# Separate views of a table in DRAM for the rows of the last three blocks, and another rhythm for the block tails at the layer seams

## The chip, the cores and the metric

One core of a Trainium2 chip runs the kernel. Its engines work side by side, each through its own list of instructions in order: PE (TensorE, matrix products), DVE (VectorE), ACT (ScalarE), POOL (GpSimd, which here mainly issues indirect DMAs) and SP (SyncE, which issues plain DMAs). Engines wait for each other, and for DMAs, by semaphores. The metric is the device time of one execution in microseconds; a kernel is given by the median of several runs.

## The reference

A graph network of four layers over 8 batches of 2048 nodes with 128 features, and one adjacency matrix, in which an entry is set with probability 0.0078, so a node has some 16 neighbours. Layers 0 and 1 are attention with 8 heads, masked by the adjacency, with a feed-forward part and two layer norms; layers 2 and 3 are graph attention (GAT):

```python
# layers 0 and 1
Q, K, V = h @ Wq, h @ Wk, h @ Wv               # 8 heads of 16
scores = einsum('bnhd,bmhd->bhnm', Q, K) / sqrt(16)
scores = where(adj == 0, -inf, scores)
attn_out = einsum('bhnm,bmhd->bnhd', softmax(scores), V)
x = layer_norm(h + (attn_out @ Wo + bo))
x = layer_norm(x + relu(x @ W1 + b1) @ W2 + b2)
# layers 2 and 3
h = x @ W
e = leaky_relu((h @ a_src)[:, :, None] + (h @ a_dst)[:, None, :], 0.2)
att = nan_to_num(softmax(where(adj == 0, -inf, e)))
x = layer_norm(einsum('bij,bjd->bid', att, h) + x)
```

## The kernel before

**Sparse work in blocks.** The kernel first turns the adjacency into lists of neighbours. Nodes are sorted by their number of neighbours into 16 blocks of 128 (`perm` holds the order), so that a block needs as many neighbour slots as its largest node has; `CAPS` gives the slots of each block, falling from 29 to 10. For every layer there is a table in DRAM, `tables[l]`, with one row for each node: its keys and values (2048 floats) for layers 0 and 1, its projected features and score terms (1040 floats) for layers 2 and 3. The slots of a block are worked through in chunks of a few slots. `gather` (L288) fetches, for one slot, one table row for each of the 128 nodes, by an indirect DMA that POOL issues: 1 MB in layers 0 and 1, 0.53 MB in layers 2 and 3. The rows land in one of 7 buffers called `kv`.

**A chunk.** `attention_chunk` (L605): the DVE multiplies keys with queries (L613) and halves the product (L619), PE adds up (L296, tile `pair`), ACT takes exponentials (L635), PE turns them (L639), ACT copies them into `weights` (L643), the DVE multiplies values with weights (L651), PE accumulates in `acc` (L296). `gat_chunk` (L764) does the like: scores on the DVE (L781), ACT scaling (L798), DVE products and sums (L793, L804), PE accumulation.

**A block's tail.** When the last chunk of a block is accumulated, `outputs` (L674) scales it on the DVE and the tail finishes the layer for the block. `attention_tail` (L699, in two halves of four batches) and `gat_tail` (L811) go back and forth between PE, for the products and layer norms (L705 to L748, L827, L303), and ACT (L462, L469, L473, L732, L835). `project` (L492) multiplies the new state with the next layer's weights (L499), and ACT copies the result to the tile `rows` (L509, and L520 to L522 for the score terms of a GAT layer, the last of them to `own`). `state_done` (L524) then keeps the state by a plain DMA of SP and calls `put_rows` (L485): an indirect DMA of POOL that scatters the 128 rows of the block into `tables[l + 1]`. These are the puts.

**The seams between layers.** A chunk of the next layer may need rows of any block. To start before all 16 blocks are put, the first two blocks of layers 1 to 3 have lists of their own, `sorted_lists`, in which neighbours that lie in early blocks come first. `EARLY` (L47) says how many of the first slots can be gathered when all but the last 3, 2 or 1 blocks are put; `fetch` (L1108) computes from it `need`, the number of puts that a chunk's gathers must follow, and issues its gathers when `put[l]` has reached that. What remains of the lists is gathered with `need` 16; among this is the chunk called folded, whose slots follow through the plain `lists`, and which is the first of the new layer that needs the put of block 15. `ORDER` (L48) is the order of these early chunks.

**Dependencies.** The program is traced in order, and a tracker puts in the waits from what each instruction reads and writes. It sees a table as one thing. So a gather waits for every put issued before it, and a put waits for every gather of this table issued before it to have landed, though it writes other rows than these read. `clear_late` (L475) has written zeros into the rows of the last three blocks at the start, so gathers never read undefined memory.

**Order of the work.** `layers` (L1188) steps through the chunks in a fixed pipeline. At several points of a step it calls `slot` (L1133): this advances each running thread by one stage (they are generators), then each running tail by one stage, then calls `fetch`; on every third call the tails get a second stage if `hurry` (L1128) says so, which is in layers 2 and 3 before all 16 puts of the layer are issued, and at one block of layer 2. The place at which a stage is traced is its place in the order of every engine that it uses.

```python
    def hurry():
        c = every[min(now[0], len(every) - 1)]
        return c["l"] == 2 and c["t"] == NT - 1 or c["l"] > 1 and put[c["l"]] < NT
```

Of the kernel before, what the change touches and what calls it, by code (L numbers as in the profile page):

```python
# [7 lines left out]

# [11 lines left out]
NT = N // P  # L20
# [24 lines left out]


EARLY = (((8, 3), (12, 2), (16, 1)), ((8, 3), (12, 1)))  # L47
ORDER = {2: ((0, 0, 12), (1, 0, 8), (0, 12, 16), (1, 8, 12)),  # L48
         4: ((0, 0, 8), (1, 0, 8), (0, 8, 16), (1, 8, 12))}
SEG = 128  # L50
# [12 lines left out]
def cut(k, end, n):  # L63

    res = []
    for m in split(end - k, n):
        res.append((k, m, False))
        k += m
    return res


def pieces(l, n):

    done, res = [0] * NT, []
    if l > 0:
        for t, k, end in ORDER[n]:
            res += [(t, *c) for c in cut(k, end, n)]
# [10 lines left out]
def sparse_path(ctx: ExitStack, tc: tile.TileContext, ins: dict, out: bass.AP, flag: bass.AP):  # L88
# [10 lines left out]
    nc = tc.nc  # L99
# [50 lines left out]
    def buffer():  # L150
        turn[0] += 1
        return bufs[turn[0] % KVB]
# [118 lines left out]
    def width(l):  # L271
        return NB * (2 * D if l < 2 else D + 2)


    tables = [dram.tile([N + (l > 1), width(l)], F32, name=f"table{l}") for l in range(4)]

    x_rows = ins["x_nodes"]


# [5 lines left out]
        nc.sync.dma_start(xT.rearrange("p b n -> p (b n)"), kept[t])  # L285
        return xT

    def gather(l, index, dst):  # L288
        nc.gpsimd.indirect_dma_start(  # L289
            out=dst, out_offset=None, in_=tables[l][:, :],  # L290
            in_offset=bass.IndirectOffsetOnAxis(ap=index, axis=0),
            bounds_check=N - (l < 2), oob_is_err=False,
        )

    def turn_into(dst, src, start):
        nc.tensor.matmul(  # L296
            dst, src, ident, start=start, stop=True, is_transpose=True, skip_group_check=True
        )
# [83 lines left out]
    def order_lists(t):  # L382
# [27 lines left out]
        yield  # L410
        for i, b in EARLY[t]:
            late = small.tile([P, 1], F32, tag="late", name="late", bufs=1)
# [62 lines left out]
    def clear_late():  # L475

        rows = rows_of(blocks[0][0])
        nc.vector.memset(rows, 0.0)
        for l in (1, 2, 3):
            for t in range(NT - 3, NT):  # L480
                for _ in range(3):
                    yield
                put_rows(l, t, rows)

    def put_rows(l, t, rows):  # L485
        nc.gpsimd.indirect_dma_start(  # L486
            out=tables[l][:, :],
            out_offset=bass.IndirectOffsetOnAxis(ap=perm[:, t : t + 1], axis=0),
            in_=rows[:, : width(l)], in_offset=None,
        )  # L490
# [33 lines left out]
    def state_done(l, t, box):  # L524


        box["halves"] = box.get("halves", 0) + 1
        if box["halves"] == 2:
            if l < 3:
                nc.sync.dma_start(kept[t], box["x"].rearrange("p b n -> p (b n)"))  # L530
                put_rows(l + 1, t, box["rows"])
                put[l + 1] += 1
            box["done"] = True
            state(l, t + STATES)
# [164 lines left out]
    def attention_tail(l, t, box, i):  # L699
# [58 lines left out]
        yield from project(l + 1, i, xT, rows_of(box), t)  # L758
        yield
        state_done(l, t, box)  # L760


# [48 lines left out]
    def gat_tail(l, t, box):  # L811
# [33 lines left out]
        def half_rows(h):  # L845
            scaled(h)
            yield
            pt = transpose4(ns[h])
            yield
            affine(xT[:, 4 * h : 4 * h + 4, :], pt, wt["col"][:, 0:2])  # L850
            yield
            yield from project(3, 4 * h, xT, rows_of(box), t)
            yield
            state_done(l, t, box)
# [15 lines left out]
        if l == 3:  # L870
            for _ in range(3):
                yield
            nc.vector.tensor_mul(n, n, last_g[:, None, :].to_broadcast([P, B, D]))
            yield
            nc.vector.tensor_add(n, n, last_b[:, None, :].to_broadcast([P, B, D]))
            yield
            nc.gpsimd.indirect_dma_start(
                out=out, out_offset=bass.IndirectOffsetOnAxis(ap=perm[:, t : t + 1], axis=0),
                in_=n.rearrange("p b d -> p (b d)"), in_offset=None,
            )  # L880
            state_done(l, t, box)
            state_done(l, t, box)
# [207 lines left out]
    put = [NT, 0, 0, 0]  # L1090
    every = []
    blocks = [[{} for _ in range(NT)] for _ in range(4)]
    for l in range(4):
        per = 2 if l < 2 else 4
        for t, k, ns, folded in pieces(l, per):
            c = dict(l=l, t=t, k=k, ns=ns, folded=folded, box=blocks[l][t])
# [3 lines left out]
    now = [0, 0]  # L1100
    beat = [0]

    def advance(group):
        for g in list(group):
            if next(g, 0) == 0:
                group.remove(g)

    def fetch():  # L1108

        while now[1] < len(every):  # L1110
            c = every[now[1]]
            l, t, k, ns = c["l"], c["t"], c["k"], c["ns"]

            if now[1] - now[0] > (5 if now[1] >= KVB and every[now[1] - KVB]["l"] > 1 else 4):
                return
            resorted = l > 0 and t < 2 and not c["folded"]
            need = NT - max([b for end, b in EARLY[t] if k + ns <= end] + [0] if resorted else [0])
            if put[l] < need:
                return
            c["buf"] = buffer()[:, : ns * width(l)].rearrange("p (s c) -> p s c", s=ns)  # L1120
            c["turn"] = turn[0]
            for i in range(ns):
                at = t * BASE if resorted else first[t]
                index = (sorted_lists if resorted else lists)[:, at + k + i : at + k + i + 1]
                gather(l, index, c["buf"][:, i])
            now[1] += 1

    def hurry():  # L1128

        c = every[min(now[0], len(every) - 1)]  # L1130
        return c["l"] == 2 and c["t"] == NT - 1 or c["l"] > 1 and put[c["l"]] < NT

    def slot():  # L1133
        advance(threads)
        advance(tails)
        fetch()
        beat[0] += 1
        if beat[0] % 3 == 0 and hurry():
            advance(tails)

    def drain():
# [20 lines left out]
    def state(l, t):  # L1162
        if t >= NT:
            l, t = l + 1, t - NT
        if 0 < l < 4:
            blocks[l][t].update(x=load_state(t), ready=True)
# [21 lines left out]
    def layers():  # L1188
        threads.append(first_states((0,)))
        drain()  # L1190
        fetch()
        begin(every[0])
        for _ in weights:
# [4 lines left out]
        for i in range(len(every) + 2):  # L1198
# [3 lines left out]
            while added:  # L1202
                c2 = added.pop(0)
                go(c2)
                if c2["last"]:
                    threads.append(tail(c2["l"], c2["t"], c2["box"]))
            now[0] = i
            fetch()
            if c["k"] == 0:
                l, t = c["l"], c["t"]  # L1210
                if l == 0:
                    if t + 2 < NT:
                        threads.append(find_lists(t + 2))
                    if t == 0:
                        threads.append(first_states(range(1, NT)))
                        threads.append(later(12, clear_late))
                    if t in (2, 6):
                        threads.append(order_lists(t // 4))
                while l < 2 and "asked" not in c["box"]:
                    slot()  # L1220
            while i < len(every) and now[1] <= i:
                slot()
# [10 lines left out]
            if c1["l"] in (2, 3) and c1["last"]:  # L1233
                sums(c1["l"], c1["t"], c1["box"])
                threads.append(scales(c1["l"], c1["box"]))
            go(c)
            slot()
            go(c)
            slot()
# [541 lines left out]
```

## Time and profile before

| | |
|---|---|
| median of 3 runs | 2844.97 us (2840.76 to 2846.59) |
| the profiled execution | 2843.96 us |
| its span in the profile | 2842.2 us |
| granted clock of TensorE, mean | 0.934 |
| busy: DVE, PE, POOL, ACT | 2520.0, 2388.3, 1753.6, 1375.9 us |
| HBM traffic over the span | 356 GB/s |
| seam from layer 0 to 1 | about 1050 to 1150 us |
| seam from layer 1 to 2 | about 1915 to 1995 us |
| seam from layer 2 to 3 | about 2385 to 2455 us |
| puts (L486) | 57, of which 48 carry rows of layers 0 to 2 and 9 are the zeros of `clear_late` |

Times are microseconds from the start of the span. In a view of groups of instructions each line names the source line, the engine, the operation, the tiles written and read, the count, the busy time and the idle time of the engine just before, with what ended it. In a view in time order each line has the start, the duration, the engine and line, and in brackets the idle time before it and what ended that, its releaser. A DMA shows twice: as the instruction of the engine that issues it, and as the wait of those who need what it moves. A releaser is the semaphore event that came last by the profile; where the engine named had long been done, another of the things waited for was the true one.

### The profile page before, as it was taken

The numbers are of one execution on the slowest core, as the hardware profiler recorded it, in microseconds if no ns is written. First come the engines' busy times: TensorE is split into PE (matmuls) and PEld (weight loads), VectorE is DVE, ScalarE is ACT, GpSimd is POOL, SyncE is SP. The second block draws the span as 40 slices with busy tenths as digits, with TensorE's granted clock in tenths as the row PEclk, the third lists the DMA queues.
The fourth block names the chain that finished last, engine by engine and source line by source line (L and its number), as shares of the span: only waits on it lengthen the run. The fifth ranks groups of instructions, "written<-read, shape, count | busy, mean of one in ns | idle before, by whom it ended". The sixth has DMA issues, their size and how long they took to land.

```text
span 2842.2 us, 49663 instructions
## 1 busy us (share of the span) xinstructions
PE 2388.3 (84%) x18176; PEld 2180.7 (77%) x18176; DVE 2520.0 (89%) x2496; ACT 1375.9 (48%) x5021; POOL 1753.6 (62%) x1276
## 2 busy tenths in 40 slices
PE   5857898899899998699989999997667887788885
PEld 3656888788788887588878888886667787777885
DVE  8888999999899897899999999985889997699995
ACT  3511444454455554154445555565345565354554
POOL 1266688678656544646565665572776775677772
PEclk9987999999999999999999999999889888999998
DMA  9698889999989878789999999984999998899994
GB/s 364 243 376 334 350 330 342 383 331 348 377 324 375 309 303 336 301 307 372 351 379 353 351 377 346 350 306 171 374 411 385 408 408 316 319 411 413 407 413 171
DMA packets 197766, 982.15 MB, mean 346 GB/s; under 512 B 30284, under 2 KB 32076, under 8 KB 125520
## 3 DMA queue, kind: packets, MB, share of 16 engines
q0 software_dynamic: 172112, 885.12, 80.7%
q1 hardware_dynamic: 20502, 75.52, 6.8%
q10 hardware_dynamic: 4900, 18.24, 1.7%
q8 instruction: 147, 2.41, 0.3%
q14 instruction: 105, 0.86, 0.1%
HBM read 921.35 MB, written 91.55 MB: 356 GB/s over the span
## 4 chain that ended last, share of the span: by engine, by line
PE 43%; DVE 22%; DMA 15%; issue 8%; ACT 6%; POOL 1%; POOLq 0%; DVEq 0%; ACTq 0%
PE acc L296 15%; DMA kv<-table,lists 10%; DVE kv L613 7%; DVE kv L651 7%; PE pair L296 4%; PE m L748 4%; PE m L727 4%; DMA kv<-table,sorted_lists 3%; PE m L303 2%; PE m L499 2%; DVE kv L793 2%; PE m L591 2%; PE m L743 2%; DVE kv L619 2%; PE m L550 2%
## 5 line engine op out<-in xcount | busy, mean ns | idle before, releaser
L289 POOL DMA_INDIRECT kv<-table,lists x938 | 1301.2, 1387 | 672.4 <-PE acc L296 327.7
L296 PE MATMUL acc<-ident,kv 128*128 128x128 f32 x8048 | 1060.5, 286 | 171.6 <-DVE kv L651 87.8
L296 PEld LDWEIGHTS acc<-ident,kv 128*128 128x128 f32 x8048 | 964.4, 149 | 241.6 <-DVE kv L651 111.8
L651 DVE TENSOR_TENSOR kv<-kv,weights 128x2048 f32<-128x2048 f32 (+1 forms) x282 | 626.1, 2220 | 61.1 <-ACT weights L643 61.0
L613 DVE TENSOR_TENSOR kv<-kv,q 128x2048 f32<-128x2048 f32 (+1 forms) x280 | 618.0, 2207 | 55.2 <-DMA kv<-table,lists 35.9
L793 DVE TENSOR_TENSOR kv<-kv,pair 128x3584 f32<-128x3584 f32 (+1 forms) x150 | 530.7, 3538 | 0.9
L296 PE MATMUL pair<-ident,kv 128*128 128x128 f32 (+1 forms) x2256 | 302.9, 279 | 89.9 <-issue 67.2
L619 DVE TENSOR_TENSOR kv<-kv 128x1024 f32<-128x1024 f32 (+1 forms) x282 | 334.7, 1187 | 9.1
L296 PEld LDWEIGHTS pair<-ident,kv 128*128 128x128 f32 (+1 forms) x2256 | 259.0, 141 | 108.4 <-issue 80.8
L643 ACT COPY weights<-pair 128x128 f32<-128x128 f32 (+1 forms) x282 | 73.2, 260 | 385.0 <-PE pair L639 378.6
L289 POOL DMA_INDIRECT kv<-table,sorted_lists x150 | 192.9, 1286 | 104.6 <-PE acc L296 36.2
L798 ACT ACTIVATE kv<-kv,ws 128x128 f32<-128x128 f32 x544 | 174.7, 397 | 170.0 <-DVE ws L787 164.8
L462 ACT ACTIVATE n<-m,eps 128x128 f32<-128x128 f32 x512 | 181.1, 371 | 149.1 <-PE m L748 145.9
L635 ACT ACTIVATE ring<-pair 128x128 f32<-128x128 f32 (+1 forms) x282 | 77.8, 276 | 319.7 <-PE pair L296 244.9
L835 ACT ACTIVATE n<-m,eps 128x128 f32<-128x128 f32 x256 | 90.6, 373 | 177.6 <-PE m L827 175.5
L486 POOL DMA_INDIRECT table<-rows,perm x57 | 90.9, 1595 | 125.7 <-ACT own L522 35.3
L748 PE MATMUL m<-w_L_w,hT 128*128 128x128 f32 x1024 | 156.4, 275 | 0.0
L469 ACT ACTIVATE n<-m,rs 128x128 f32<-128x128 f32 x512 | 145.8, 374 | 0.1
L748 PEld LDWEIGHTS m<-w_L_w,hT 128*128 128x128 f32 x1024 | 135.2, 192 | 0.0
L727 PE MATMUL m<-n1T,w_L_gnn_W 128*128 128x512 f32 x256 | 132.0, 599 | 1.5 <-ACT hT L732 1.4
L303 PE MATMUL m<-ident,n 128*128 128x128 f32 x640 | 112.2, 291 | 12.5 <-ACT n L469 6.4
L499 PE MATMUL m<-w_L_h,xT 128*128 128x130 f32 x512 | 83.3, 294 | 40.0 <-ACT xT L473 25.8
(220 smaller groups left out, 3685.1 us busy)
## 6 DMA issues: line engine op xcount, KB each, us to landing
kept<-xT SPq DMA_DIRECT2D x48, 512.0 KB, 6.7
xT<-kept SPq DMA_DIRECT2D x48, 512.0 KB, 7.0
kv<-in_adj_dram SPq DMA_DIRECT2D x16, 1024.0 KB, 9.4
table<-kv ACTq DMA_DIRECT2D x16, 1024.0 KB, 5.2
kv<-table,lists POOLq DMA_INDIRECT x938, 8.6
kv<-in_x_nodes_dram SPq DMA_DIRECT2D x16, 512.0 KB, 6.6
kv<-table,sorted_lists POOLq DMA_INDIRECT x150, 7.1
found<-cand POOLq DMA_DIRECT2D x16, 64.0 KB, 6.1
```

Source lines behind the costliest of these rows:

```text
L289: nc.gpsimd.indirect_dma_start(out=dst, out_offset=None, in_=tables[l][:, :], in_offset=bass.IndirectOffsetOnAxis(ap=index, axis=0), bound ...
L296: nc.tensor.matmul(dst, src, ident, start=start, stop=True, is_transpose=True, skip_group_check=True)
L303: nc.tensor.transpose(pt[:, j * P : (j + 1) * P], src[:, j, :], ident)
L462: nc.scalar.activation(dst[:, i, :], z[:, i, :], AF.Square, bias=eps, scale=D**-0.5, accum_out=ss[:, i : i + 1],)
L469: nc.scalar.mul(dst[:, i, :], z[:, i, :], rs[:, i : i + 1])
L613: nc.vector.tensor_mul(kk, kk, q[:, None].to_broadcast([P, ns, NB, D]))
L619: nc.vector.tensor_add(hk.rearrange("p j (c h) -> p c j h", h=NH), kj[:, :, :NH, :], kj[:, :, NH:, :])
L651: nc.vector.tensor_mul(vv, vv, w.rearrange("p (s b h) -> p (s b) h", b=NB, h=NH)[:, :, None, :] .to_broadcast([P, ns * NB, HD, NH]),)
L727: nc.tensor.matmul(ph, wt["1"][:, f * P : (f + 1) * P], n1T.rearrange("p b c -> p (b c)"), start=True, stop=True,)
L748: nc.tensor.matmul(y[:, j, :], hT[:, f, j, :], wt["2"][:, f, :], start=False, stop=f == 1, skip_group_check=True,)
L793: nc.vector.tensor_mul(hv[:, :, :nv, :], hv[:, :, :nv, :], wc[:, :, :nv, None].to_broadcast([P, ns, nv, D]))
L798: nc.scalar.mul(hv[:, i, b, :], hv[:, i, b, :], ws[:, i, b - nv : b - nv + 1])
```

## The change

Two things are changed.

First, the tables of layers 1 to 3 get views which the tracker holds to be disjoint from each other, while the table itself still overlaps them all: view 0 for the rows of blocks 0 to 12, and one for each of the blocks 13, 14 and 15 (`LATE = 3`). Each view is the whole table as far as addresses go. `put_rows` writes through the view of its block. A gather with `need` under 16 reads through view 0, and is given by hand a dependency on the puts of those blocks from 13 on that it does need; a gather with `need` 16 reads through the table. With this, the puts of blocks 13 to 15 no longer wait for early gathers, and early gathers don't wait for puts that they don't need.

Second, `slot` advances the tails a second time on every call, not every third, while the layer of the current chunk is at least 1 and not all 16 puts of its table are issued. This holds at all three seams; `hurry` had held for layers 2 and 3.

```diff
@@ -3,6 +3,7 @@
 import concourse.bass as bass
 import concourse.tile as tile
 from concourse import mybir
+from concourse.ap import dram_disjoint_views
 from concourse.masks import make_identity
 from concourse._compat import with_exitstack
 
@@ -45,6 +46,7 @@
 
 
 EARLY = (((8, 3), (12, 2), (16, 1)), ((8, 3), (12, 1)))
+LATE = 3
 ORDER = {2: ((0, 0, 12), (1, 0, 8), (0, 12, 16), (1, 8, 12)),
          4: ((0, 0, 8), (1, 0, 8), (0, 8, 16), (1, 8, 12))}
 SEG = 128
@@ -274,6 +276,9 @@
 
     tables = [dram.tile([N + (l > 1), width(l)], F32, name=f"table{l}") for l in range(4)]
 
+    views = {l: dram_disjoint_views(tables[l][:, :], 1 + LATE) for l in (1, 2, 3)}
+    puts = {l: [] for l in (1, 2, 3)}
+
     x_rows = ins["x_nodes"]
 
 
@@ -285,12 +290,19 @@
         nc.sync.dma_start(xT.rearrange("p b n -> p (b n)"), kept[t])
         return xT
 
-    def gather(l, index, dst):
-        nc.gpsimd.indirect_dma_start(
-            out=dst, out_offset=None, in_=tables[l][:, :],
+    def gather(l, index, dst, need):
+        this = nc.gpsimd.indirect_dma_start(
+            out=dst, out_offset=None, in_=tables[l][:, :] if need == NT else views[l][0],
             in_offset=bass.IndirectOffsetOnAxis(ap=index, axis=0),
             bounds_check=N - (l < 2), oob_is_err=False,
         )
+        if need < NT:
+            for other in puts[l][NT - LATE : need]:
+                tc.add_manual_dep(
+                    this.ins, other.name,
+                    mybir.DependencyInfo(mybir.DependencyClass.Sync, mybir.DependencyReason.DATA),
+                    reason="rows of a block before",
+                )
 
     def turn_into(dst, src, start):
         nc.tensor.matmul(
@@ -482,9 +494,9 @@
                     yield
                 put_rows(l, t, rows)
 
-    def put_rows(l, t, rows):
-        nc.gpsimd.indirect_dma_start(
-            out=tables[l][:, :],
+    def put_rows(l, t, rows, dst=None):
+        return nc.gpsimd.indirect_dma_start(
+            out=tables[l][:, :] if dst is None else dst,
             out_offset=bass.IndirectOffsetOnAxis(ap=perm[:, t : t + 1], axis=0),
             in_=rows[:, : width(l)], in_offset=None,
         )
@@ -528,7 +540,9 @@
         if box["halves"] == 2:
             if l < 3:
                 nc.sync.dma_start(kept[t], box["x"].rearrange("p b n -> p (b n)"))
-                put_rows(l + 1, t, box["rows"])
+                dst = views[l + 1][max(0, t - (NT - LATE) + 1)]
+                assert len(puts[l + 1]) == t
+                puts[l + 1].append(put_rows(l + 1, t, box["rows"], dst).ins)
                 put[l + 1] += 1
             box["done"] = True
             state(l, t + STATES)
@@ -1122,7 +1136,7 @@
             for i in range(ns):
                 at = t * BASE if resorted else first[t]
                 index = (sorted_lists if resorted else lists)[:, at + k + i : at + k + i + 1]
-                gather(l, index, c["buf"][:, i])
+                gather(l, index, c["buf"][:, i], need)
             now[1] += 1
 
     def hurry():
@@ -1135,7 +1149,8 @@
         advance(tails)
         fetch()
         beat[0] += 1
-        if beat[0] % 3 == 0 and hurry():
+        c = every[min(now[0], len(every) - 1)]
+        if c["l"] > 0 and put[c["l"]] < NT or beat[0] % 3 == 0 and hurry():
             advance(tails)
 
     def drain():
```

## The prediction

> **What bounds the kernel.** I read the page first: which engine is busy, and where the traffic sinks.
>
> ```profile
> PE 2388.3 (84%) x18176; PEld 2180.7 (77%) x18176; DVE 2520.0 (89%) x2496; ACT 1375.9 (48%) x5021; POOL 1753.6 (62%) x1276
> ...
> GB/s 364 243 376 334 350 330 342 383 331 348 377 324 375 309 303 336 301 307 372 351 379 353 351 377 346 350 306 171 374 411 385 408 408 316 319 411 413 407 413 171
> ...
> L486 POOL DMA_INDIRECT table<-rows,perm x57 | 90.9, 1595 | 125.7 <-ACT own L522 35.3
> ```
>
> The DVE is the busiest engine at 89%, but the bandwidth row has a hole: 171 in its 28th slice, which is 1918 to 1990 us, where layer 1 ends and layer 2 begins. The last line is the puts (L486), the scatters of a finished block's rows into the next layer's table: 57 of them, with POOL idle 125.7 us before them. A put is cheap to issue, so what it waits for is the question. Next, busy time by stretch (PE, PEld, DVE, ACT, POOL, then clock, DMA share and GB/s):
>
> ```profile
> 1150.00:1250.00 100.00, 78.91 (x608) 70.12 (x609) 95.46 (x57) 31.58 (x114) 56.90 (x34) 0.94 0.85 312
> ...
> 1985.00:2350.00 365.00, 276.64 (x2010) 260.98 (x2011) 338.19 (x398) 190.72 (x758) 277.93 (x250) 0.85 1.00 394
> 2350.00:2445.00 95.00, 72.58 (x546) 68.20 (x545) 63.27 (x70) 51.14 (x205) 43.31 (x41) 0.86 0.76 283
> 2445.00:2790.00 345.00, 280.11 (x2322) 271.82 (x2321) 310.15 (x373) 162.65 (x632) 260.31 (x255) 0.94 1.02 408
> ```
>
> In layers 2 and 3 the gather stream is the limit (DMA share 1.00 and 1.02, 394 and 408 GB/s). At the seam from layer 2 to layer 3 the share drops to 0.76. At the start of layer 1 the DVE is the limit (95.46 of 100 us). Past each seam some resource is saturated, so what a seam gains or loses is passed on whole; what it gains is when the next layer's stream can start. Then POOL in time order at the seam from layer 2 to 3 (start, duration, line, idle before and its end):
>
> ```profile
> 2390.35 0.99 POOL L289 DMA_INDIRECT kv<-table,sorted_lists  x1 [0.30 <-issue]
> 2399.57 1.02 POOL L486 DMA_INDIRECT table<-rows,perm  x1 [8.22 <-DMA kv<-table,sorted_lists]
> 2403.74 1.01 POOL L289 DMA_INDIRECT kv<-table,sorted_lists  x1 [3.16 <-DMA table<-rows,perm]
> ...
> 2416.21 1.02 POOL L486 DMA_INDIRECT table<-rows,perm  x1 [7.57 <-ACT kv L798]
> 2420.38 1.01 POOL L289 DMA_INDIRECT kv<-table,sorted_lists  x1 [3.15 <-DMA table<-rows,perm]
> ...
> 2439.35 1.02 POOL L486 DMA_INDIRECT table<-rows,perm  x1 [8.90 <-DMA kv<-table,sorted_lists]
> 2443.49 1.01 POOL L289 DMA_INDIRECT kv<-table,lists  x1 [3.12 <-DMA table<-rows,perm]
> ```
>
> Puts of blocks 13, 14 and 15. Each sits until the early gathers in front of it have landed (8.22, 7.57, 8.90 us), then goes out into an empty queue, and the next gather waits for it to land (3.16, 3.15, 3.12). The releaser of the second is named ACT, but that had long been done; the gathers were outstanding. The rows themselves were ready sooner: the last ACT write (L522) ends at 2383.8, 2409.5 and 2427.3. The other two seams:
>
> ```profile
> 1136.66 2.53 POOL L486 DMA_INDIRECT table<-rows,perm  x1 [16.33 <-DMA kv<-table,sorted_lists]
> ...
> 1949.78 1.02 POOL L486 DMA_INDIRECT table<-rows,perm  x1 [15.96 <-ACT own L522]
> ...
> 1980.45 1.02 POOL L486 DMA_INDIRECT table<-rows,perm  x1 [16.44 <-ACT own L522]
> ```
>
> The first is block 15 from layer 0 to 1: it waits 16.33 us for gathers, with its rows ready at 1118.4. The next two, blocks 14 and 15 from layer 1 to 2, wait for something else: ACT's own last copy, ended 1949.6 and 1980.2. So at this seam it is the block's tail that is late. What the DVE loses behind them, again by its timeline:
>
> ```profile
> 1117.18 2.29 DVE L613 TENSOR_TENSOR kv<-kv,q 128x2048 f32<-128x2048 f32 x1 [4.18 <-DMA kv<-table,sorted_lists]
> ...
> 1149.54 2.29 DVE L613 TENSOR_TENSOR kv<-kv,qf 128x2048 f32<-128x2048 f32 x1 [7.79 <-DMA kv<-table,lists]
> ...
> 1992.75 0.17 DVE L781 TENSOR_TENSOR kv<-kv,mine 128x16 f32<-128x16 f32 x1 [17.18 <-DMA kv<-table,lists]
> ...
> 2450.92 0.17 DVE L781 TENSOR_TENSOR kv<-kv,mine 128x16 f32<-128x16 f32 x1 [8.08 <-DMA kv<-table,lists]
> ```
>
> and the puts' own view, what POOL waited for, who waited for the put, and its time to landing:
>
> ```profile
>   ACT own L522: 35.3, 3
>   DMA kv<-table,sorted_lists: 33.5, 3
> ...
>   ACT rows L509: 19.3, 3
> ...
> DMA to landing us min/median/max: 3.4/8.5/12.0
> ```
>
> A put alone lands 3.4 us after issue; those sent into a filled queue take 8.5 at the median, 12.0 at most.
>
> **The change, part by part.** Nothing is added on any engine: matmuls, DVE, ACT, POOL and SP instructions are as many as before, and DVE's and SP's order is the same. POOL's order differs at one seam only, layer 0 to 1: puts 14 and 15 each go ahead of 6 gathers. What changes besides is which waits the last three puts carry (before all eight gather lanes and ACT; after one lane and ACT) and the order of ACT and PE at the three seams.
>
> *Seam 2 to 3, the views.* Put 13 no longer waits 8.22 us and goes at 2391.65, right behind the gather of 2390.35 (1.30 us pace). But that gather's packets still stand in the same queue, and the put of before started only when they had landed, at 2399.5. In a filled stream a further 0.53 MB costs 1.3 us (411 GB/s), against 3.46 us for a put sent alone (2399.57 to 2403.03). So it lands at about 2401.0, 2.0 us sooner, not 8.2. ACT's L509 copy, held 7.88 us for this put until 2403.05, moves with it, so do the gathers of 2403.74 and rows 14. Put 14 gains the same on top (3.46 against 1.4), put 15 again: 2.0, 4.0, 6.0 us. The fold chunk of the DVE comes at 2444.9 instead of 2450.92. Bounds: nothing, if the queue keeps the fixed part anyway; 8.22 + 7.57 + 8.90 = 24.7 us, if puts pass the gathers in flight. I take 6.0: the 8.5 us median landing in filled queues is near the first case, far from the second.
>
> In the Trainium skill, "DMA: Bandwidth & Descriptors", section "Queues, rings and completion order", each DMA engine takes the descriptors of a ring in order. This speaks against the change: an early issue buys no place ahead of the gathers. By it the seam gives these 6.0 us; without it 24.7. The 8.5 us median agrees.
>
> *Seam 1 to 2, tails at two stages a beat.* Views give nothing here, since puts 14 and 15 wait for ACT's rows. PE was full from 1919 to 1972 and mixes the tails with the chunks' accumulations; in the new order 48 accumulating matmuls that stood ahead of block 15's last projection (L499) come behind it (24 for block 14). Twelve of them took 1.47 us at 1914.79, so 48 x 0.122 = 5.9 us. The put goes at 1974.5 and the stream starts 5.9 us sooner. The displaced matmuls run in PE's hole of 17 us while the DVE waits (17.18 us before 1992.75); were that hole gone, they would cost their 5.9. Bounds: 0, if the tail is a ping-pong of PE and ACT in which the matmuls only filled gaps; 17.18 is all that there is to lose. I take 5.9, as PE shows no gaps there.
>
> *Seam 0 to 1, both.* Here the stage behind is the DVE's. After 1098 the DVE waits 17.0 us in all: 2.17 + 1.19 for weights, 4.18 for gathers, 1.38 + 0.28, and 7.79 for the fold chunk behind put 15. Put 15 could go at about 1117 instead of 1136.66, so the data waits can go. Against it, the doubled tail pushes chunk work back on PE: 48 accumulations and 27 pair matmuls pass behind the tail, and the chunks' softmax sums (L639) come up to 12.7 us later in the middle of the seam (PE's order summed at 0.599 us for wide, 0.22 for narrow and 0.11 for accumulating matmuls), back to 0 at the end of it. PE is full from 1045 to 1119.7, so this is real delay, and weights (ACT) and DVE queue behind it. Laying DVE's unchanged order (5.69 us a chunk) against that, the fold chunk comes at 1147.8 instead of 1149.54: 1.7 us gained of 17.0. Bounds: 17.0 gained, if PE's lateness hides; 12.7 lost, if the waits stay. I take 1.7, the hand-laid order.
>
> Sum: 6.0 + 5.9 + 1.7 = 13.6 us. The profiled execution took 2843.96 (span 2842.2 and 1.8 around it) and comes to 2830.4; it lies 1.0 below the median of the runs, 2844.97, so I predict **2831**.
>
> **Rivals.**
> *A, the views bring nothing, the tails do.* A put's packets go out behind the gathers, and its fixed time still follows the last of them: seam 2 to 3 gives 0, seam 0 to 1 gives 0, only the 5.9 remain: 2839. For it: no row shows the fixed 3.4 us of a lone landing overlapped. Against: the three puts at seam 2 to 3 go out after the queue has run empty, and that at least ends.
> *B, puts overtake the gathers.* Seam 2 to 3 then gives the whole 24.7, with 5.9 and 1.7 that is 32.3: 2813. For it: the 8.5 us median may come from puts behind the 1 MB gathers of layers 0 and 1, and no row of before shows a put behind early gathers of 0.53 MB. Against: the same packets share one queue, and 12.0 us is the worst.
> *C, starved chunks: slower.* The tails' second stage comes before the chunks' matmuls, so weights come late and, as PE's accumulations are what POOL mostly waits on for free kv buffers (300 waits of L289, 363.9 us in the list of waits), the gathers too. Seam 0 to 1 then loses 12.7 with its waits still paid, seam 1 to 2 gives back its 5.9, and seam 2 to 3 keeps 6.0 less the 32 accumulations that go behind block 15's tail there (3.9): 12.7 - 2.1 = 10.6 slower, 2856. It decides once gathers at seam 0 to 1 start later than before, not only the DVE. For it: PE is full there. Against: after 1119.7 PE has room to catch up.
> *D, the change does not do what it says:* the one lane left in the puts' waits stands for a late gather, or ACT is late instead. All seams as before: 2844 to 2845.
>
> **Chances.** Forecast 0.58 (its own range 2824 to 2838), A 0.13, B 0.07, C 0.12, D 0.10. The range 2819 to 2846 leaves out B and C, 0.19. A measurement here tells 0.2% (5.7 us) from nothing: faster is below 2839.3, slower above 2850.7. A lies at that bound and is split. Faster: 0.58 + 0.07 + 0.06 = 0.71. Same: 0.10 + 0.07 = 0.17. Slower: C, 0.12.
>
> **What would show it.** Right: POOL's idle before the puts at seam 2 to 3 gone (none above 2 us released by gathers), their landing times up to about 9 us, the fold chunk about 6 us nearer to the seam's start. At seam 1 to 2 the DVE's 17.18 us shrinks by about 6 and puts 14 and 15 still wait for ACT's L522, sooner. At seam 0 to 1 the 7.79 and 4.18 us for data shrink while waits of the DVE on ACT weights and PE pairs grow to about 15 us. Wrong: these weight waits above 20 us (C), puts landing within 4 us of issue (B), or puts still idle on gathers (D).

## The result, and the profile after

The changed kernel takes 2833.40 us (median of 22 runs, 2825.11 to 2838.68), the kernel before in runs beside it 2841.77 us (22 runs, 2832.07 to 2849.07). The ratio is 0.9971, 95% interval 0.9963 to 0.9979: some 8 us faster. In a later comparison on another chip it was 0.9960 (0.9946 to 0.9974). The profiled execution took 2833.26 us, its span 2831.5, 10.7 less than the span before.

The page of the changed kernel, its busy times, its bandwidth by slices and its puts, which now stand in line 498 (gathers are in 294, the DVE's key products in 627, the weights' product in 665, the tail's scaling in 688, the GAT scores in 795):

```profile
PE 2394.6 (85%) x18176; PEld 2181.0 (77%) x18176; DVE 2520.7 (89%) x2496; ACT 1376.6 (49%) x5021; POOL 1749.0 (62%) x1276
...
GB/s 359 249 376 334 353 333 343 379 336 343 382 328 353 322 313 301 312 317 356 347 380 370 342 366 366 349 298 199 356 411 399 400 409 338 343 411 413 405 413 170
...
L498 POOL DMA_INDIRECT table<-rows,perm x57 | 94.8, 1663 | 68.7 <-ACT own L534 17.3
```

Busy times are as before. POOL's idle time before its puts fell from 125.7 to 68.7 us, yet only a fifth of these 57 us came off the span. Where it went shows in POOL's order of time at the seam from layer 2 to 3 (start, duration, what it is, idle time before and its end):

```profile
2387.88 0.99 POOL L294 DMA_INDIRECT kv<-table,sorted_lists  x1 [0.30 <-issue]
2389.17 1.02 POOL L498 DMA_INDIRECT table<-rows,perm  x1 [0.30 <-ACT n L857]
2398.82 1.01 POOL L294 DMA_INDIRECT kv<-table,sorted_lists  x1 [8.62 <-DMA table<-rows,perm]
...
2402.73 0.99 POOL L294 DMA_INDIRECT kv<-table,sorted_lists  x1 [0.30 <-issue]
2404.05 1.02 POOL L498 DMA_INDIRECT table<-rows,perm  x1 [0.33 <-ACT own L534]
2412.96 1.01 POOL L294 DMA_INDIRECT kv<-table,sorted_lists  x1 [7.89 <-issue]
...
2422.07 0.99 POOL L294 DMA_INDIRECT kv<-table,sorted_lists  x1 [0.30 <-issue]
2423.37 1.02 POOL L498 DMA_INDIRECT table<-rows,perm  x1 [0.30 <-ACT kv L812]
2432.43 1.01 POOL L294 DMA_INDIRECT kv<-table,lists  x1 [8.05 <-PE acc L308]
```

The three waits of 8.22, 7.57 and 8.90 us ahead of the puts are gone: each put follows a gather or its own rows within 0.33 us. But the next gather on POOL, called the put's follower below, needs the put's rows, and it now starts 9.65, 8.91 and 9.06 us after the put, where it was 4.17, 4.17 and 4.14. Most of the wait has moved from before the put to behind it. The puts of block 15 at the other two seams:

```profile
1120.00 1.02 POOL L498 DMA_INDIRECT table<-rows,perm  x1 [3.04 <-ACT rows L517]
1121.32 2.27 POOL L294 DMA_INDIRECT kv<-table,sorted_lists  x1 [0.31 <-PE acc L308]
...
1978.15 1.02 POOL L498 DMA_INDIRECT table<-rows,perm  x1 [14.05 <-ACT own L534]
1984.98 1.01 POOL L294 DMA_INDIRECT kv<-table,lists  x1 [5.82 <-DMA table<-rows,perm]
```

At seam 0 to 1 put 15 waits 3.04 us for its rows instead of 16.33 for gathers, and gathers follow at once. At seam 1 to 2 it still waits for ACT, goes at 1978.15 instead of 1980.45, and then the next gather takes 6.83 us to come, not 4.92. The view of the puts' line has their times from issue to landing:

```profile
DMA to landing us min/median/max: 5.0/8.3/13.2
```

No put lands in 3.4 us any more: the shortest takes 5.0. And the DVE, in order of time over the three seams (the lines at 1151.06, 1992.44 and 2439.74 are the fold chunks):

```profile
1067.82 2.29 DVE L665 TENSOR_TENSOR kv<-kv,weights 128x2048 f32<-128x2048 f32 x1 [6.92 <-ACT weights L657]
1079.21 1.29 DVE L688 TENSOR_TENSOR o<-acc,scale 128x512 f32<-128x512 f32 x2 [5.64 <-PE acc L308]
...
1113.81 2.29 DVE L665 TENSOR_TENSOR kv<-kv,weights 128x2048 f32<-128x2048 f32 x1 [5.32 <-ACT weights L657]
...
1151.06 2.28 DVE L627 TENSOR_TENSOR kv<-kv,qf 128x2048 f32<-128x2048 f32 x1
...
1992.44 0.18 DVE L795 TENSOR_TENSOR kv<-kv,mine 128x16 f32<-128x16 f32 x1 [14.31 <-DMA kv<-table,lists]
...
2439.74 0.18 DVE L795 TENSOR_TENSOR kv<-kv,mine 128x16 f32<-128x16 f32 x1 [5.15 <-DMA kv<-table,lists]
```

At seam 0 to 1 the data waits of the DVE (7.79 and 4.18 us among others) are gone, the fold chunk starts without any wait, but waits for ACT's weights and PE's accumulations have come up, and it starts at 1151.06 instead of 1149.54.

DVE's instructions come in the same order in all kernels of this study but for their waits, so one can look up the same instruction in two traces and subtract the starts. The median of these differences ahead of a seam, subtracted from their value around the seam's fold chunk, gives what the seam gained, to some tenths of a microsecond. Below, us (plus is later): the changed kernel against the profile of before; its second profile against one of the kernel before on that chip; and the two profiles of the kernel before against each other, in which up to 1.5 us is chance:

```
                 changed   changed again   before again
seam 0 to 1       +1.2         +1.8            +0.1
seam 1 to 2       -2.6         -2.0            +0.7
seam 2 to 3       -8.6         -4.3            -1.5
```

Around 1225 us, past the fold chunk of seam 0 to 1, both profiles of the changed kernel fall back another 1.6 us, which is not in these figures.

### The profile page after: what moved, and what is told of

It is laid out like the page before. It is cut to its first block, busy times and chain, and to the rows that moved or that the text cites. A ratio compares the mean times of both kernels' runs of the same rounds, so it can differ in the third digit from the quotient of the medians.

```text
span 2831.5 us, 49678 instructions
## 1 busy us (share of the span) xinstructions
PE 2394.6 (85%) x18176; PEld 2181.0 (77%) x18176; DVE 2520.7 (89%) x2496; ACT 1376.6 (49%) x5021; POOL 1749.0 (62%) x1276
## 4 chain that ended last, share of the span: by engine, by line
PE 43%; DVE 22%; DMA 14%; issue 7%; ACT 7%; POOL 1%; POOLq 0%; DVEq 0%; ACTq 0%
PE acc L308 14%; DMA kv<-table,lists 11%; DVE kv L627 7%; DVE kv L665 7%; PE pair L308 4%; PE m L762 4%; PE m L741 4%; PE m L315 3%; PE m L511 3%; DVE kv L633 2%; PE m L757 2%; PE m L605 2%; PE m L564 2%; DVE kv L807 2%; PE m L724 2%
## 5 line engine op out<-in xcount | busy, mean ns | idle before, releaser
L294 POOL DMA_INDIRECT kv<-table,lists x938 | 1282.6, 1367 | 681.4 <-PE acc L308 343.4
L633 DVE TENSOR_TENSOR kv<-kv 128x1024 f32<-128x1024 f32 (+1 forms) x282 | 334.8, 1187 | 9.1
L498 POOL DMA_INDIRECT table<-rows,perm x57 | 94.8, 1663 | 68.7 <-ACT own L534 17.3
```

The lines of the kernel that those rows point to most:

```text
L294: this = nc.gpsimd.indirect_dma_start(out=dst, out_offset=None, in_=tables[l][:, :] if need == NT else views[l][0], in_offset=bass.Indirec ...
L633: nc.vector.tensor_add(hk.rearrange("p j (c h) -> p c j h", h=NH), kj[:, :, :NH, :], kj[:, :, NH:, :])
```

## The experiments

**Parts of the change.** Four kernels, run beside the kernel before on one chip. On this chip layers 2 and 3 are slower for every kernel (363 GB/s from 2085 to 2350 us in the first of them, 402 in the trace of before), with medians near 2949 us; layers 0 and 1 are not. So ratios are compared within this chip, seams 0 to 1 and 1 to 2 with the trace of before, and seam 2 to 3 with the run that has no views. In layer 2 of this chip the differences between two kernels wander by several us, so its figures for seam 2 to 3 are good to 3 or 4 us only.

Views only: the change with its second part undone.

```diff
-        c = every[min(now[0], len(every) - 1)]
-        if c["l"] > 0 and put[c["l"]] < NT or beat[0] % 3 == 0 and hurry():
+        if beat[0] % 3 == 0 and hurry():
```

> The views with the tails' old rhythm (a second stage on every third call, in layers 2 and 3 only). Theory A, the parts add up seam by seam: seam 2 to 3 keeps most of the 8.7 us that the changed kernel gained there; seam 1 to 2 gives 0; at seam 0 to 1 put 15 goes right after its 6 gathers are issued (about 1121 instead of 1136.66) and PE's order is the old one, so the DVE loses its data waits of 4.18 and 7.79 us without the 18 us of lateness seen in the changed kernel: 8 to 12 us gained there. About 16 to 20 us faster than before, some 0.9935, faster than the changed kernel. Rival B, the two parts need each other: with the old rhythm the puts stand behind gathers in POOL's list, seam 0 to 1 gives at most 3 and seam 2 to 3 some 6: about 0.9970, like the changed kernel or slower.

Measured: 0.9960 (0.9941 to 0.9980). At seam 0 to 1 the lead goes from 1.7 us behind to 6.0 ahead: 7.7 us gained, where the changed kernel loses 1.2 to 1.8. At seam 1 to 2 it loses 2.9, at seam 2 to 3 it gains 9.8 against the rhythm alone. POOL at seam 0 to 1:

```profile
1120.45 3.06 POOL L498 DMA_INDIRECT table<-rows,perm  x1 [1.37 <-ACT rows L517]
1136.45 2.41 POOL L294 DMA_INDIRECT kv<-table,lists  x1 [12.94 <-DVE kv L633]
```

Put 15 goes at 1120.45 instead of 1136.66, as expected, with no change of the tails; the gather behind it has the DVE's L633, by which a buffer comes free, as its releaser, so it is no longer the put that holds it. So the views do their work there without the rhythm. Of theory A, that the parts add up, the mechanism at seam 0 to 1 holds, with 7.7 us where it set 8 to 12. Seam 1 to 2 loses 2.9 where it set nothing, which is not explained, and 0.9960, some 12 us, lies between both theories' figures.

Rhythm only: the kernel before with the new condition in `slot`, no views.

```diff
-        if beat[0] % 3 == 0 and hurry():
+        c = every[min(now[0], len(every) - 1)]
+        if c["l"] > 0 and put[c["l"]] < NT or beat[0] % 3 == 0 and hurry():
```

> The new rhythm with one table and no views. Theory A: seam 0 to 1 loses, since the chunks come late and puts 14 and 15, now ahead of 6 gathers, still wait for all gathers issued before to land: 3 to 10 us slower there; seam 1 to 2 gains the 2.7 seen; seam 2 to 3 within 1 us: together 1 to 6 us slower than before, about 1.0012. Rival B: the rhythm is what brings the puts forward, seam 0 to 1 loses no more than the 1.6 of the changed kernel and seam 1 to 2 gains 2.7: about 0.9995.

Measured: 1.0025 (1.0006 to 1.0045), slower. Seam 0 to 1 loses 6.0 us (2.7 ahead, then 3.3 behind), seam 1 to 2 gains 1.6. POOL around put 15 at seam 0 to 1:

```profile
1112.94 1.05 POOL L289 DMA_INDIRECT kv<-table,sorted_lists  x1 [4.32 <-PE acc L296]
1120.83 2.00 POOL L486 DMA_INDIRECT table<-rows,perm  x1 [6.84 <-ACT weights L643]
1127.19 1.30 POOL L289 DMA_INDIRECT kv<-table,sorted_lists  x1 [4.36 <-PE pair L639]
```

The put was brought ahead of 6 gathers, but with one table it still waits 6.84 us. ACT's last copy of its rows (L505) ends at 1116.75, so 4.1 us of this are for the gathers before it, though the releaser named is another. The chunks pay for the tails and little comes back. This is theory A, which set a loss of 3 to 10 us for the seam.

The rhythm from seam 1 to 2 on, with views everywhere:

```diff
-        if c["l"] > 0 and put[c["l"]] < NT or beat[0] % 3 == 0 and hurry():
+        if c["l"] > 1 and put[c["l"]] < NT or beat[0] % 3 == 0 and hurry():
```

> The views, and the new rhythm at seams 1 to 2 and 2 to 3 only; seam 0 to 1 has the old one. Theory A: seam 0 to 1 gains 8 to 12 us as in the run with views alone, seam 1 to 2 gains 2.7, seam 2 to 3 gains 8.7: 19 to 23 us faster than before, about 0.9925, the best of the four. Rival B: seam 0 to 1 gives at most 3 us: about 0.9950. A second rival: the chunks of seam 0 to 1 are late in any order, and the DVE's waits only change their names: about 0.9960.

Measured: 0.9945 (0.9922 to 0.9968). Seam 0 to 1 gains 6.3, less than the 8 to 12 of theory A and more than the 3 of its rival. And the rhythm at seam 1 to 2 alone, `c["l"] == 2` in the same place:

> The views, and the new rhythm at seam 1 to 2 only; seam 2 to 3 has the old rhythm, a second stage on every third call. Theory A: as the run with the new rhythm from seam 1 to 2 on, within 1.5 us, since at seam 2 to 3 the puts' waits and not the tails were late: about 0.9930. Rival: the tails' rhythm is part of the 8.7 us of seam 2 to 3 (its last put brought 3.7, the others 2.4 and 2.5): 2 to 4 us slower than that run.

Measured: 0.9941 (0.9920 to 0.9962), seam 0 to 1 gains 6.1, seam 2 to 3 gains 6.6 against 7.0 with the rhythm, and the medians of the two kernels are 2932.51 and 2932.52 us: no difference that these runs can tell. But this run's lead falls from 11.5 us at 2300 us to 8.1 at 2380, shortly before the seam; read at the first of these its gain is 3.1, so a part of some 3 us for the rhythm there is not excluded.

The traces of this chip also show what sets a put's landing. Here the rows at seam 2 to 3 came late, so puts went out at different times after the last gather. Views only, POOL:

```profile
2422.56 0.99 POOL L294 DMA_INDIRECT kv<-table,sorted_lists  x1 [0.30 <-issue]
2423.86 1.02 POOL L498 DMA_INDIRECT table<-rows,perm  x1 [0.31 <-issue]
2432.91 1.01 POOL L294 DMA_INDIRECT kv<-table,sorted_lists  x1 [8.03 <-DMA table<-rows,perm]
...
2436.81 0.99 POOL L294 DMA_INDIRECT kv<-table,sorted_lists  x1 [0.30 <-issue]
2440.45 1.02 POOL L498 DMA_INDIRECT table<-rows,perm  x1 [2.65 <-ACT own L534]
2446.54 1.01 POOL L294 DMA_INDIRECT kv<-table,sorted_lists  x1 [5.07 <-PE acc L308]
```

A put 1.30 us behind the last gather has its follower 9.05 us later; one 3.64 us behind, 6.09 us later. In the run with the rhythm at seam 1 to 2 alone the puts are 1.30 and 5.02 us behind, and their followers come 9.42 and 5.45 later. These four sums are 10.35, 9.73, 10.72 and 10.47: with gaps up to some 5 us the follower comes some 10 to 12 us after the last gather was issued, whenever the put itself went. In the changed kernel the three sums are 10.94, 10.23 and 10.36, and in its second profile, below, 11.44, 10.30 and 11.22. With longer gaps the sum grows, and there is a floor, 4.14 to 4.17 us in the kernel before, with gaps of 8.56 to 9.89. This is what the order in one queue gives; that the load on the DMA engines, and not the order, delays the put was not separated from it.

**All on one chip.** The kernel before was profiled again beside the changed kernel and two others, for the comparison by seams.

> The kernel before, profiled on the same chip as the three runs beside it, so that the seams can be compared on one chip. Fold chunks of the DVE after waits of about 7.8, 17.2 and 8.1 us; put 15 to the next gather 6.9, 4.9 and 4.1 us.

Measured: 2844.12 us; the followers at seam 2 to 3 come 4.17, 4.16 and 4.14 us after the puts.

> The changed kernel on the same chip as the runs beside it: 0.9965 to 0.9975 of the kernel before. Seam 0 to 1 loses 1 to 2 us, seam 1 to 2 gains 2 to 3, seam 2 to 3 gains 8 to 9.

Measured: 0.9960 (0.9946 to 0.9974), 2832.48 us beside 2842.65. Seams 0 to 1 and 1 to 2 as expected; seam 2 to 3 gained 4.3 in this execution, not 8 to 9, though its puts are followed after 10.14, 9.00 and 9.92 us, within a microsecond or so of the first profile. This execution took 2838.59 us, the longest of its five. Some 2.8 us of the difference were lost before any of the three puts went: against the kernel before on this chip, the gathers are issued 2.0 us sooner at 2349 us and 0.8 us later at 2388. From the last gather ahead of each put to its follower, the first profile of the changed kernel saves 2.45, 2.50 and 3.67 us, 8.6 in all, and the second 1.85, 2.22 and 3.04, 7.1 in all.

> Views at all seams, the new rhythm from seam 1 to 2 on, beside the changed kernel on one chip. Theory (the rhythm costs the 7 to 8 us at seam 0 to 1 by which the first measurement of this kernel came to the fold chunk sooner): 0.9945, and 6 to 8 us below the changed kernel, all of it at seam 0 to 1. Rival (that difference was the other chip's): within 2 us of the changed kernel.

Measured: 0.9933 (0.9919 to 0.9947), 2824.26 us: 8.2 us below the changed kernel. Seams: 6.1, 3.5 and 6.5 us gained. So at seam 0 to 1 leaving out the rhythm is worth 7.9 us on this chip (6.1 gained, 1.8 lost). Its DVE there:

```profile
1105.84 2.29 DVE L665 TENSOR_TENSOR kv<-kv,weights 128x2048 f32<-128x2048 f32 x1 [2.16 <-ACT weights L657]
...
1112.78 2.34 DVE L665 TENSOR_TENSOR kv<-kv,weights 128x2048 f32<-128x2048 f32 x1 [1.19 <-ACT weights L657]
...
1143.61 2.29 DVE L627 TENSOR_TENSOR kv<-kv,qf 128x2048 f32<-128x2048 f32 x1 [4.24 <-PE acc L308]
```

The first two are the only waits for weights above half a microsecond that are left, where the changed kernel has 6.92 and 5.32 us among others: 3.6 us in all against 14.9. The tail's wait of 5.64 us for accumulations is down to 1.64. The fold chunk, the third line, starts at 1143.61; what is left ahead of it is a wait for PE's accumulations.

Next, why the put of seam 1 to 2 lands late. SP's and POOL's order of time in the changed kernel, second profile:

```profile
1976.64 0.32 SPq L542 DMA_DIRECT2D kept<-xT  x1
1979.30 0.32 SPq L290 DMA_DIRECT2D xT<-kept  x1
```

```profile
1979.06 1.02 POOL L498 DMA_INDIRECT table<-rows,perm  x1 [15.72 <-ACT own L534]
1985.84 1.01 POOL L294 DMA_INDIRECT kv<-table,lists  x1 [5.76 <-DMA table<-rows,perm]
```

SP writes the state of block 15 and, once that is done, loads another block's state into the same buffer, 512 KB each. That load goes out 0.24 us after the put. In the six profiles with the new rhythm so far it went 0.24 to 0.26 us behind this put, and the follower came 6.7 to 6.8 us after the put. With the old rhythm the load went ahead of the put, by 1.06 us in both profiles of the kernel before (follower after 4.9) and by 0.41 with views only (5.4). The next kernel has the views and the rhythm from seam 1 to 2 on, with this load held at all three seams until the put has landed:

```diff
+        this = nc.sync.dma_start(xT.rearrange("p b n -> p (b n)"), kept[t])
+        if after is not None:
+            tc.add_manual_dep(this.ins, after.name, ...)
...
-            state(l, t + STATES)
+            state(l, t + STATES, puts[l + 1][t] if l < 3 and t == NT - 1 else None)
```

> As e3_again, but the load of a kept state that SP issues at each seam after block 15 waits until put 15 has landed. In the runs with the new rhythm put 15 at seam 1 to 2 goes out within 0.3 us of this load (1978.15 and 1978.39) and the next gather comes 6.7 to 6.8 us after the put; with the old rhythm 4.9 to 5.4. Theory, the two transfers share the DMA engines: the next gather comes 4.2 to 5.0 us after put 15, and all later work 1.8 us sooner, 0.9939. Rival, the longer landing has another cause: 6.7 us stays and the time is that of e3_again within 1 us.

Measured: 0.9925 (0.9912 to 0.9939), 2821.03 us; the follower comes after 4.23 us, seam 1 to 2 gains 5.0. In time it is 3.2 us below the same kernel without this hold, with intervals that overlap. So the time alone doesn't decide; the follower does, for the theory that the two transfers are in each other's way.

**Further steps.** Three kernels on a third chip.

> The kernel with views, the new rhythm from seam 1 to 2 on and the state's load behind put 15, once more, beside the two built on it: 0.9925 of the kernel before. Put 15 to the next gather 4.2 us at seam 1 to 2 if the load was the cause of 6.7; 6.7 if the first measurement was chance.

Measured: 0.9908 (0.9890 to 0.9926). SP and POOL at seam 1 to 2:

```profile
1964.57 0.32 SPq L548 DMA_DIRECT2D kept<-xT  x1
1970.43 0.32 SPq L290 DMA_DIRECT2D xT<-kept  x1
```

```profile
1966.99 1.02 POOL L504 DMA_INDIRECT table<-rows,perm  x1 [14.04 <-ACT own L540]
1971.21 1.01 POOL L300 DMA_INDIRECT kv<-table,lists  x1 [3.21 <-PE acc L314]
```

The load goes at 1970.43, after the put's landing, and the gather at 1971.21, 4.22 us after the put. It was not chance. Then the tails' second stage on every third call at seam 0 to 1:

```diff
-        if c["l"] > 1 and put[c["l"]] < NT or beat[0] % 3 == 0 and hurry():
+        if c["l"] > 1 and put[c["l"]] < NT or beat[0] % 3 == 0 and (hurry() or c["l"] == 1 and put[1] < NT):
```

> As e5_again, with a second stage for the tails on every third call at seam 0 to 1, where the changed kernel has it on every call and e5_again on none. Theory, at this seam any tail work put ahead costs the chunks as much PE time as it moves, and the DVE is the limit there: the fold chunk comes 1 to 4 us later than in e5_again, 0.993 to 0.994. Rival, only doubling on every call overdoes it and a third of it pulls put 15 forward without a late DVE: 1 to 2 us sooner than e5_again, 0.992.

Measured: 0.9902 (0.9885 to 0.9918), 2818.99 us beside 2821.19: no difference that these runs can tell. Seam 0 to 1 gains 6.6 where the run beside it gains 6.3, so a third of the rhythm does not cost what the whole costs, and the theory, that any tail work costs the chunks as much, fails in its size. That it is 1 to 2 us better, as the rival has it, is not shown either. And three stages at seam 1 to 2:

```diff
             advance(tails)
+            if c["l"] == 2 and put[2] < NT:
+                advance(tails)
```

> As e5_again, with three stages of the tails on each call at seam 1 to 2, where put 15 still waits some 15 us for ACT's last copy and the DVE 12.7 us for the gathers behind it. Theory, the tail there is held by accumulations of chunks that PE does in between, each 24 of them 2.6 to 2.9 us: one more group goes behind the tail and put 15 comes 2 to 3 us sooner, 0.9917. Rival, after two stages the tail is a ping-pong of PE and ACT with gaps of its own: rows come no sooner than in e5_again, within 1 us, 0.9925 or worse.

Measured: 0.9912 (0.9896 to 0.9928), 2821.77 us. POOL's puts of blocks 14 and 15 there:

```profile
1934.14 1.02 POOL L504 DMA_INDIRECT table<-rows,perm  x1 [13.52 <-ACT own L540]
1941.92 1.02 POOL L300 DMA_INDIRECT kv<-table,sorted_lists  x1 [6.76 <-PE m L321]
...
1967.09 1.02 POOL L504 DMA_INDIRECT table<-rows,perm  x1 [14.49 <-ACT own L540]
```

```profile
1934.05 0.32 SPq L290 DMA_DIRECT2D xT<-kept  x1
```

Put 14 waits 13.52 us for ACT instead of 15.87 and goes 2.9 us sooner than in the kernel beside it (1934.14 against 1937.03). But its follower comes 7.78 us after it instead of 5.25, so the follower is only 0.4 us sooner, at 1941.92. The last view shows a likely reason: SP's load of a state, which is held back at block 15 alone, goes 0.09 us ahead of this put. Put 15 goes at 1967.09 where it went at 1966.99. By its time the rival holds, a third stage brings nothing for block 15; but its reason, that rows come no sooner, is not what block 14 shows. Whether the third stage would pay with the load held back there too was not run.

Views at all seams, the rhythm from seam 1 to 2 on and the load behind the put, the kernel of these that was timed twice, beats both kernels: 22 and 25 us below the kernel before by the medians of its two comparisons, where the change as made gives 8 and 10.

## Why the prediction was right, and where it was off

The direction was right and the time in the range: 2831 foretold, 2833.40 measured. The gain was 13.6 us in the sum, and 8.4 by the medians (10.2 in the second comparison). That the time came within 2.4 us of the forecast is in part luck. The kernel before ran at 2841.77 us in the longer comparison, 3.2 below the 2844.97 from which the forecast started, which makes up for a good half of the 5.2 us of gain that were missing. And by seams the gains were 8.6, 2.6 and -1.2 us in the first profile, where 6.0, 5.9 and 1.7 had been put: one seam gave more than its term and two gave less. By steps:

*Seam 2 to 3, 6.0 us.* 8.6 and 4.3 us in the two profiles of the changed kernel, 6.5 in the mean, and some 5 to 9 in the others on chips of that speed. The mechanism is as put: the waits of 8 us ahead of the puts are not the gain, since a put issued early stands behind the gathers. The prediction has put 13 land at 2401.0, 9.35 us after its issue at 2391.65, and landings up to about 9 us; followers came after 9.65, 8.91 and 9.06. What each put saves was put at 2.0 us and measured 2.45, 2.50 and 3.67 in the first profile and 1.85, 2.22 and 3.04 in the second, so the seam's 6.0 us were some 1 to 3 us too small. The rule of the Trainium skill, page "DMA: Bandwidth & Descriptors", section "Queues, rings and completion order", that a ring's descriptors are taken in order, agrees with these and with the sums of 10 to 12 us above; the section says it of the queues of SP and ACT, and the puts and gathers are on POOL's. Of the 4.3 us between the two profiles, 1.5 lie in these savings and the rest in gathers that came late ahead of put 13 in the second; why they did is not settled. Rival B, puts that overtake, needed landings near 4 us behind gathers and falls. Rival A, that the views bring nothing, falls by the same seam and by the run with views alone.

*Seam 1 to 2, 5.9 us.* 2.6 and 2.0. The step that failed is "the put goes at 1974.5 and the stream starts 5.9 us sooner": it took the put's landing over from the trace of before. Two terms were mis-sized. The rows came 2.3 us sooner in absolute time (1977.97 against 1980.27) in a trace that was 2.4 us behind at the seam's start, so 4.7 us instead of 5.9. The prediction's ground, that PE shows no gaps there, is not what the trace of before has: PE was busy 47.5 of the 53 us from 1919 to 1972 and waited 2.35 and 1.18 us for ACT (L469) before its instructions at 1947.40 and 1965.87. That the missing 1.2 us lie in these gaps is not shown. And the put moved beside the state's load and took 1.9 us longer to be followed. SP's order did not change, as the prediction says, but what lay beside its transfer did. With that load held back and two stages a call the seam gives 5.0 to 5.4 us in three profiles, which is close to the term. In the Trainium skill the same section has each DMA engine take turns between the queues it has work for. By this alone, as an estimate, the put's 1.3 us of data would take 1.3 us more beside a load of the same size; the traces have 2.5 more (6.7 to 6.8 against 4.2), so the direction agrees and the size does not.

*Seam 0 to 1, 1.7 us.* A loss of 1.2 to 1.8, and from 1225 us on 1.6 more. The wrong step is the size of the delay in "the fold chunk comes at 1147.8": the data waits did go, 12.3 us to none, but waits for weights went from 3.6 to 14.8 and for accumulations from 1.7 to 5.6, so DVE was up to 18.0 us late, from 1113.81 on, where PE's order alone had given 12.7. The first two of these waits, 6.92 and 5.64 us at 1067.82 and 1079.21, come ahead of the stretch after 1098 for which the prediction lists the waits. The prediction's signs for this were right (data waits gone, weight waits "about 15 us"); the sum of it was 3 us too good. What it did not see is that the two parts pull in opposite directions here: without the rhythm the views give 6 to 8 us, and the rhythm takes 6 to 8 back.

*Rivals C and D.* C has the right place and mechanism, a starved chunk pipeline at seam 0 to 1, and with the rhythm alone its direction comes true (1.0025), with 6.0 us lost at the seam instead of its 12.7. With the views its sign, that gathers start later than before, holds for the early gathers and fails for those that need put 15. In the kernel before, the first of the six that put 15 now passes, and the first behind it that reads the plain lists, are these:

```profile
1110.67 0.99 POOL L289 DMA_INDIRECT kv<-table,sorted_lists  x1 [0.30 <-issue]
...
1143.54 1.01 POOL L289 DMA_INDIRECT kv<-table,lists  x1 [4.35 <-PE pair L639]
```

In the changed kernel the first of them is the one at 1121.32, 10.7 us later, and the second is this, 10.5 us sooner:

```profile
1133.07 1.89 POOL L294 DMA_INDIRECT kv<-table,lists  x1 [0.30 <-PE pair L308]
```

What C has wrong is its price, 12.7 us lost "with its waits still paid": the data waits went, and the loss was 1.2 to 1.8. D falls: no put at seam 2 to 3 waits over 0.33 us.

## What to carry to other kernels

If a transfer waits for others on its own queue, taking the wait away may save only a part of it, because the transfer then stands in the queue; here some 2 to 4 us of the 7.6 to 8.9 for each put. Before a tail is hurried ahead of the work that feeds the next stage, ask which resource that stage is short of: here it paid where the next stage waited for rows, and cost as much as the views had brought where the next stage was the DVE's. And when work moves in time, list what other queues send in the same microseconds: a 512 KB load of another queue beside the last put took back 2 us of a gain of 5.

## What the runs showed of the hardware that was not expected

A 512 KB load from SP's queue, sent 0.24 us after a 0.53 MB scatter of POOL with the last gather issued some 17 us before, went with a follower of the scatter after 6.78 us; with the load held back it came after 4.22 and 4.23. And one chip moved 363 GB/s in the gather-bound stretch of layer 2, where the first moved 402, and every kernel took some 100 us longer on it, in layers 2 and 3 and not in layers 0 and 1.
